# Dispatching tokens to experts by scattering rows into per-expert DRAM regions, block by block

## The chip, the cores and the metric

One core of a Trainium2 chip runs the whole program. The metric is the device time of one execution in microseconds (us); of several runs the median is taken. The engines are named as in the profile: PE (TensorE, matrix multiply), DVE (VectorE), ACT (ScalarE), POOL (GpSimd) and SP (SyncE, which here only issues DMAs). Each engine takes its own instructions in order, so an instruction that waits holds up all that stand behind it on the same engine.

## The reference

Two transformer layers with adaptive layer norm over 2048 tokens of 128 channels, fp32. The part that the change touches is the second half of layer 0, a mixture of experts:

```
x = x + ga * attention0(h)                      # 16 heads of 8, no mask
h = layernorm(x) * (1 + cb) + sb
logits = h @ router_w.T                         # 16 experts
top_vals, top_idx = top_k(logits, 1)            # one expert per token
scores = sigmoid(scattered top_vals)            # 0 for the experts not chosen
routed_in = h * scores                          # per expert
gate, up = split(routed_in @ gate_up_proj)      # 128 -> 2 x 128 per expert
expert_sum = sum over experts of (up * silu(gate)) @ down_proj
shared = silu(h @ shared_gate_w.T) * (h @ shared_up_w.T) @ shared_down_w.T   # 512 wide
x = x + gb * (shared + expert_sum)
```

Layer 1 follows with causal attention (8 heads of 16 that share one key and value head) and a channel mix with a one-token shift.

## The kernel before, in words

The tokens are kept transposed as channels by tokens (`hT`) for matrix products, and as 16 tiles of 128 tokens (`x`) for everything by row. The 2048 tokens are also seen as four blocks of 512 (`b` = 0 to 3).

**Attention 0.** The work is cut into 16 units, one for each block of queries and group of four heads. Each unit has a first pass, 32 steps that compute scores (L377) and take their maximum (L381), and a second pass, 32 steps that compute the scores again with the maximum subtracted (L442), exponentiate (L452) and weigh the values (L468). The order is written by hand: while the second pass of unit u runs, the first pass of unit u+1 is issued between its steps, 8 steps (`LEAD`) ahead. At the end of a first pass the function `turn` transposes the maxima, ACT copies them (`mT`, L411), and two DMAs on the SP queue (L414) write them into rows of the stacked queries `qS`. The scores of the unit's second pass read those rows, so they wait for these two DMAs. The queries of block 1 are put into `qS` by 32 further SP DMAs (`project_q`, lines at L260), issued in the first pass of unit 1. In unit 1's second pass SP also writes zeros (L358) when unit 0's scores are all done.

A list `late` holds small pieces of other work. One is taken off it every other step, and every step in the last unit. It starts with one piece (`fold0`); in the last unit it gets the pieces of `route(b)` for blocks 0 to 2, and those of block 3 run after the unit. `route(b)` normalises block b, transposes it, computes the router's logits (L707), the largest logit `top`, and a one-hot choice `mine` (L714).

**The expert stage.** Rows of `h` are transposed, multiplied with the sigmoid of `top` and written to DRAM (`hs_rows`, L782, SP). A second path works out where each token goes: 17 matmuls of `mine` with triangular and all-one matrices give its position inside its expert (`pos`, L842 to L846), DVE makes from the counts the number of 128-row tiles of each expert and their first slot (`over`, `base`, L851 to L858), and 16 matmuls (L890) invert this to a table `tok` of the token in every slot. There are 31 tiles (`SLOTS`), enough for any split of 2048 tokens over 16 experts. POOL then issues 31 indirect DMAs (L912), each gathering 128 rows of `hs_rows` by `tok`; slots that no token fills read row 0. Eight quads of four tiles follow: transposes of the rows (L921), gate and up products with the expert's weights (L935), the activation (L804 to L806), the down product (L948) and a copy to `y` (L952), stored by SP to `y_rows` (L953). The expert's number of each tile is read into a register of PE, one load per tile (L929). Pieces of the shared expert (L826, L814) are put between the quads. At the end 16 indirect DMAs (L970) gather each token's row of `y_rows` and add it to `x`. The gate `gb` is folded into both down weights by two POOL multiplications (L791).

SP issues its DMAs in order, over eight rotating completion counters: a DMA that reuses a counter first waits until the DMA eight places before it has landed.

Of the kernel before, what the change touches and what calls it, by code (L numbers as in the profile page):

```python
# [18 lines left out]
P = 128  # L19
# [10 lines left out]
SHARED_FIRST = 4  # L30
LEAD = 8
# [11 lines left out]
def two_layers(ctx: ExitStack, tc: tile.TileContext, a: dict, out: bass.AP):  # L43
# [91 lines left out]
    for i, at in enumerate((ident.rearrange("p (r c) -> p r c", c=4)[:, :, 2:4],  # L135
# [4 lines left out]
    nc.gpsimd.memset(zeros, 0.0)  # L140

# [4 lines left out]
    units = const.tile([P, P], F32, name="units")  # L146
    nc.gpsimd.iota(units, pattern=[[1, P]], base=0, channel_multiplier=0,
                   allow_small_or_imprecise_dtypes=True)
    token = const.tile([P, NT], F32, name="token")
    nc.gpsimd.iota(token, pattern=[[P, NT]], base=0, channel_multiplier=1,  # L150
# [135 lines left out]
    def attention(layer, hT, ngrp, dk, scale, causal, kvp, begin, prepare, wq, bq, folded, ended,  # L286
# [22 lines left out]
        with ExitStack() as s:  # L309
# [10 lines left out]
            def other_bank():  # L320
                return banks[(weighing + 1) % 2]
# [209 lines left out]
            if not folded:  # L531
                late.append(lambda: folded.extend(fold0(other_bank())))

# [160 lines left out]
    ranked = const.tile([P, NT, NE], F32, name="ranked")  # L694
    best = const.tile([P, NT], F32, name="best")
    mine = const.tile([P, NT, NE], F32R, name="mine")

    def route(b, bank):
        got = []
        cols = slice(HOFF + b * QB, HOFF + (b + 1) * QB)  # L700
        ts = slice(b * TB, (b + 1) * TB)

        def choose():
            ps = bank()[:, :TB * NE].rearrange("p (t e) -> p t e", e=NE)
            for i in range(TB):
                lo = HOFF + b * QB + i * P
                nc.tensor.matmul(ps[:, i, :], h1[:, lo:lo + P], wr0, start=True, stop=True)  # L707
            nc.vector.tensor_reduce(top[:, ts], ps, AX.X, ALU.max)
            r = ranked[:, ts, :]
            nc.vector.tensor_tensor(r, ps, top[:, ts].unsqueeze(2).to_broadcast([P, TB, NE]),  # L710
                                    ALU.is_equal)
            nc.vector.tensor_tensor(r, r, rank.unsqueeze(1).to_broadcast([P, TB, NE]), ALU.mult)
            nc.vector.tensor_reduce(best[:, ts], r, AX.X, ALU.max)
            nc.vector.tensor_tensor(mine[:, ts, :], r,  # L714
                                    best[:, ts].unsqueeze(2).to_broadcast([P, TB, NE]),
                                    ALU.is_equal)

        return [lambda: got.extend(moments(b, f"ln1{b}")),
                lambda: got.append(normal(b, f"ln1{b}", *got)),
                lambda: turn_normal(bank(), got[2], h1[:, cols], m[:, 4:5], m[:, 3:4]),  # L720
                choose]
# [10 lines left out]

    def ended0(bank):
        return ([lambda: folded1.extend(fold_gate(const, bank(), wo1, vcol(V_BP),
                                                  mods[1][:, 2:3], "a1"))]
                + [p for b in range(NB - 1) for p in route(b, bank)])
# [3 lines left out]
    a0.close()  # L740

# [14 lines left out]
    with ExitStack() as s:  # L756
# [10 lines left out]
        topsig = rp.tile([P, NT], F32, name="topsig")  # L767
        nc.scalar.activation(topsig, top, AF.Sigmoid)


        hs = rp.tile([P, NT, P], F32, name="hs")
        hs_v = a["hs_rows"].rearrange("(t p) c -> p t c", p=P)
        for b in range(NB):
            ps = pt.tile([P, QB], F32, name=f"hs_ps{b}", tag="t")
            for i in range(TB):
                t = b * TB + i
                nc.tensor.transpose(ps[:, i * P:(i + 1) * P], hT[:, t * P:(t + 1) * P], ident)
            for i in range(TB):
                t = b * TB + i
                nc.scalar.activation(hs[:, t, :], ps[:, i * P:(i + 1) * P], AF.Copy,  # L780
                                     scale=topsig[:, t:t + 1])
            nc.sync.dma_start(out=hs_v[:, b * TB:(b + 1) * TB, :],  # L782
                              in_=hs[:, b * TB:(b + 1) * TB, :])

# [4 lines left out]
        nc.scalar.copy(gb, ps[:, :P])  # L789
        for w, n in ((wsd, NS), (wdn, NE)):  # L790
            nc.gpsimd.tensor_tensor(w, w, gb.unsqueeze(1).to_broadcast([P, n, P]), ALU.mult)  # L791
# [5 lines left out]
        def silu_up(ps, n, name):  # L797
# [6 lines left out]
            nc.scalar.activation(v[0], g, AF.Sigmoid)  # L804
            nc.vector.tensor_tensor(v[0], v[0], g, ALU.mult)
# [27 lines left out]
        def shared_step():  # L833
            up = shared_up()
            if waiting:
# [3 lines left out]
        first = [shared_up()]  # L839


        pos = pt.tile([P, NT + 1, NE], F32, name="pos_ps", tag="t")  # L842
        nc.tensor.matmul(pos[:, :NT, :], before_r, mine, start=True, stop=False,
                         skip_group_check=True)
        for t in range(NT):
            nc.tensor.matmul(pos[:, t + 1:, :], ones_r,  # L846
                             mine[:, t:t + 1, :].to_broadcast([P, NT - t, NE]),
                             start=False, stop=(t == NT - 1), skip_group_check=True)
        first.append(shared_up())
        over = rp.tile([P, NE, NE], F32, name="over")  # L850
        nc.vector.tensor_tensor(over, pos[:, NT, :].unsqueeze(2).to_broadcast([P, NE, NE]),  # L851
# [7 lines left out]
        place = rp.tile([P, NT, NE], F32, name="place")  # L859
        nc.vector.tensor_tensor(place, pos[:, :NT, :],  # L860
                                base.unsqueeze(1).to_broadcast([P, NT, NE]), ALU.add)
        nc.vector.tensor_tensor(place, place, mine.bitcast(F32), ALU.mult)
        slot = rp.tile([P, NT], F32, name="slot")
        nc.vector.tensor_reduce(slot, place, AX.X, ALU.add)
        slot_i = rp.tile([P, NT], I32, name="slot_i")
        nc.vector.tensor_copy(slot_i, slot)
        hi_i = rp.tile([P, NT], I32, name="hi_i")
        nc.vector.tensor_scalar(hi_i, slot_i, 7, 7, ALU.arith_shift_right, ALU.arith_shift_left)
        hi = rp.tile([P, NT], F32, name="hi")
        nc.vector.tensor_copy(hi, hi_i)  # L870
        lo = rp.tile([P, NT], F32, name="lo")
        nc.vector.tensor_tensor(lo, slot, hi, ALU.subtract)


        NSL = SLOTS + 1
        in_tile = rp.tile([P, NT, NSL], F32, name="in_tile")
        nc.vector.tensor_tensor(in_tile, hi.unsqueeze(2).to_broadcast([P, NT, NSL]),
                                iota[:, :NSL].unsqueeze(1).to_broadcast([P, NT, NSL]),
                                ALU.is_equal)
        in_tile_r = rp.tile([P, NT, NSL], F32R, name="in_tile_r")  # L880
        nc.vector.tensor_tensor(in_tile_r, in_tile,
                                token.unsqueeze(2).to_broadcast([P, NT, NSL]), ALU.mult)
        at = rp.tile([P, NT, P], F32R, name="at")
        ps = pt.tile([P, NSL], F32, name="tok_ps", tag="t")
        for b in range(NB):
            cols = slice(b * TB, (b + 1) * TB)
            nc.vector.tensor_tensor(at[:, cols, :], lo[:, cols].unsqueeze(2).to_broadcast([P, TB, P]),
                                    units.unsqueeze(1).to_broadcast([P, TB, P]), ALU.is_equal)
        for t in range(NT):
            nc.tensor.matmul(ps, at[:, t, :], in_tile_r[:, t, :], start=(t == 0),  # L890
                             stop=(t == NT - 1))
        tok = rp.tile([P, NSL], U32, name="tok")
        nc.vector.tensor_copy(tok, ps)

# [3 lines left out]
        nth = rp.tile([1, SLOTS], F32, name="nth")  # L898
        nc.vector.tensor_reduce(nth, passed[:, :, 1:], AX.X, ALU.add)
        expert = rp.tile([1, SLOTS], I32, name="expert")  # L900
        nc.vector.tensor_copy(expert, nth)

        for up in first:
            shared_act(*up)
# [4 lines left out]
        quads = [list(range(j, min(j + TB, SLOTS))) for j in range(0, SLOTS, TB)]  # L909
        xs = rp.tile([P, SLOTS, P], F32, name="xs")  # L910
        for j in range(SLOTS):
            nc.gpsimd.indirect_dma_start(  # L912
                out=xs[:, j, :], out_offset=None, in_=a["hs_rows"],
                in_offset=bass.IndirectOffsetOnAxis(ap=tok[:, j:j + 1], axis=0))
        y_v = a["y_rows"].rearrange("(j p) c -> p j c", p=P)
        xsT, gup, acts, actT, regs = {}, {}, {}, {}, {}
# [9 lines left out]
        def gathered(q):  # L926
            xsT[q] = turned([xs[:, j, :] for j in quads[q]], len(quads[q]), f"xsT{q}")
            for j in quads[q]:
                regs[j] = nc.tensor.value_load(expert[0:1, j:j + 1], min_val=0, max_val=NE - 1)  # L929
# [14 lines left out]
        def down(q):  # L944
# [7 lines left out]
            nc.vector.tensor_copy(y[:, :n, :].rearrange("p j f -> p (j f)"), ps[:, :n * P])  # L952
# [53 lines left out]
        def bank():  # L1006
            return pt.tile([P, QB], F32, name="a1bank", tag="t")
# [122 lines left out]
```

## Time and profile before

| what | value |
| --- | --- |
| median of 3 runs | 1295.77 us (1295.49 to 1297.65) |
| the profiled execution's own time | 1296.39 us |
| span of the profiled execution, first to last instruction | 1294.7 us |
| mean granted PE clock | 0.933 |
| PE busy | 1166.7 us (90%) |
| DVE busy | 958.2 us (74%) |
| ACT busy | 776.4 us (60%) |
| POOL busy | 112.3 us (9%) |
| bytes moved by DMA | 27.38 MB |

The span starts with loads and the first norm, attention 0 fills about 92 to 812 us, the router of the last block and the expert stage about 812 to 978 us, then attention 1 and the channel mix follow. All times in the text count from the start of the span. Busy shares are averages over these stages, so what a part of the change is worth has to be read in its own stage. A name like `a0qS<-a0mT` in a line gives what is written and what is read, and `<-` behind an idle time gives what ended it. In the rows by stretch of time, each engine's busy us stand with their number of instructions, then the granted clock, the mean busy share of the 16 DMA engines, and GB/s.

### The profile page before, as it was taken

The numbers are of one execution on the slowest core, as the hardware profiler recorded it, in microseconds if no ns is written. First come the engines' busy times: TensorE is split into PE (matmuls) and PEld (weight loads), VectorE is DVE, ScalarE is ACT, GpSimd is POOL, SyncE is SP. The second block draws the span as 40 slices with busy tenths as digits, with TensorE's granted clock in tenths as the row PEclk, the third lists the DMA queues.
The fourth block names the chain that finished last, engine by engine and source line by source line (L and its number), as shares of the span: only waits on it lengthen the run. The fifth ranks groups of instructions, "written<-read, shape, count | busy, mean of one in ns | idle before, by whom it ended". The sixth has DMA issues, their size and how long they took to land.

```text
span 1294.7 us, 22355 instructions
## 1 busy us (share of the span) xinstructions
PE 1166.7 (90%) x9243; PEld 528.8 (41%) x9243; DVE 958.2 (74%) x1494; ACT 776.4 (60%) x857; POOL 112.3 (9%) x173
## 2 busy tenths in 40 slices
PE   5579999999999999999999999854977999999986
PEld 3233443444334344334434434533643444444432
DVE  4788888989888898898898841531468779897225
ACT  6117777777777777777777787401312355656763
POOL 2010000000000000000000000253041111100113
PEclk9659999999999999999999999876976799999998
DMA  4831000000000010000000000413211001000001
GB/s 127 112 37 34 3 2 2 2 19 18 1 2 2 3 34 2 2 2 2 2 2 1 2 2 1 131 38 34 57 31 33 19 15 29 7 1 1 2 1 32
DMA packets 25317, 27.38 MB, mean 21 GB/s; under 512 B 5328, under 2 KB 18896, under 8 KB 24704
## 3 DMA queue, kind: packets, MB, share of 16 engines
q1 hardware_dynamic: 21440, 20.50, 7.4%
q0 software_dynamic: 1504, 3.08, 1.6%
q10 hardware_dynamic: 2272, 2.36, 0.8%
q8 instruction: 73, 1.20, 0.4%
q14 instruction: 28, 0.23, 0.1%
HBM read 9.88 MB, written 4.13 MB: 11 GB/s over the span
## 4 chain that ended last, share of the span: by engine, by line
PE 77%; DVE 11%; ACT 4%; issue 3%; another core or an unknown queue 2%; DMA 1%; POOL 1%; POOLq 0%; ACTq 0%; DVEq 0%; SPq 0%
PE a0bank L468 23%; PE a0p L442 17%; PE a0p L377 12%; PE a1bank L468 5%; PE a1p L442 4%; DVE a0mx L381 3%; PE a1p L377 2%; DVE a1mx L381 2%; PE a1p L448 2%; DVE a1masked L386 2%; PE sg L826 2%; ACT a0e L452 1%; PE gu L935 1%; PE a0bank L499 1%
## 5 line engine op out<-in xcount | busy, mean ns | idle before, releaser
L381 DVE TENSOR_REDUCE a0mx<-a0p 128x2 f32<-128x1024 f32 x512 | 623.6, 1224 | 78.0 <-PE a0p L377 68.4
L452 ACT ACTIVATE a0e<-a0p 128x1024 f32<-128x1024 f32 x512 | 521.7, 1024 | 172.5 <-PE a0p L442 147.2
L468 PE MATMUL a0bank<-a0e,vA 128*32 128x256 f32 x4096 | 333.6, 392 | 0.6 <-ACT a0e L452 0.6
L377 PE MATMUL a0p<-kS,a0qS 64*128 64x512 f32 x1024 | 248.2, 481 | 26.4 <-DVE a0mx L381 13.4
L442 PE MATMUL a0p<-a0qS,kS 64*128 64x512 f32 x1024 | 259.8, 497 | 0.0
L452 ACT ACTIVATE a1e<-a1p 128x1024 f32<-128x1024 f32 (+3 forms) x160 | 143.1, 896 | 97.4 <-PE a1p L448 94.4
L442 PEld LDWEIGHTS a0p<-a0qS,kS 64*128 64x128 f32 x1024 | 97.1, 184 | 204.3 <-issue 128.8
L377 PEld LDWEIGHTS a0p<-kS,a0qS 64*128 64x128 f32 x1024 | 100.3, 192 | 111.3 <-ACT a0e L452 58.1
L468 PEld LDWEIGHTS a0bank<-a0e,vA 128*32 128x32 f32 x4096 | 86.4, 108 | 139.2 <-issue 124.9
L381 DVE TENSOR_REDUCE a1mx<-a1p 128x2 f32<-128x1024 f32 x96 | 115.6, 1222 | 20.8 <-PE a1p L377 19.9
L468 PE MATMUL a1bank<-a1e,vA 128*32 128x256 f32 (+1 forms) x1152 | 97.5, 385 | 0.5 <-POOL a1e L455 0.4
L442 PE MATMUL a1p<-a1qS,kS 64*128 64x512 f32 (+3 forms) x320 | 76.4, 472 | 3.1 <-DVE a1mx L381 1.9
L377 PE MATMUL a1p<-kS,a1qS 64*128 64x512 f32 (+3 forms) x320 | 68.3, 429 | 7.1 <-DVE a1mx L386 4.1
L386 DVE CUSTOM_DVE_ANT_0 a1masked<-a1p,later 128x128 f32<-128x128 f32 (+3 forms) x128 | 62.5, 489 | 13.3 <-PE a1p L377 8.5
L977 POOL MEMSET vA<- 128x16 f32 x1 | 0.1, 128 | 718.4 <-PE a0bank L520 718.4
L448 PE MATMUL a1p<-a1mT,a1ones 64*128 64x512 f32 (+3 forms) x320 | 61.8, 378 | 0.0
L442 PEld LDWEIGHTS a1p<-a1qS,kS 64*128 64x128 f32 x320 | 31.1, 190 | 60.9 <-issue 33.4
L377 PEld LDWEIGHTS a1p<-kS,a1qS 64*128 64x128 f32 x320 | 32.7, 199 | 36.1 <-DVE a1mx L386 10.3
L455 POOL TENSOR_SCALAR_AFFINE_SELECT a1e<-a1e 128x256 f32<-128x256 f32 x64 | 26.0, 406 | 233.7 <-ACT a1e L452 233.7
L468 PEld LDWEIGHTS a1bank<-a1e,vA 128*32 128x32 f32 x1152 | 25.4, 108 | 43.0 <-issue 32.8
L935 PE MATMUL gu<-wgu_sb,xsT 128*128 x62 | 18.5, 451 | 20.0 <-issue 19.5
L411 ACT CAST a0mT<-a0bank 8x512 fp32r<-8x512 f32 x16 | 9.2, 574 | 45.4 <-PE a0bank L410 45.3
(330 smaller groups left out, 795.7 us busy)
## 6 DMA issues: line engine op xcount, KB each, us to landing
kS<-a0qS SPq DMA_DIRECT2D x28, 128.0 KB
wgu_sb<-in_gate_up SPq DMA_DIRECT2D x1, 2048.0 KB
a0qS<-a0qh SPq DMA_DIRECT2D x62, 32.0 KB
a0qS<-a0ql SPq DMA_DIRECT2D x62, 32.0 KB
y_rows<-y SPq DMA_DIRECT2D x7, 256.0 KB
a1qS<-a1qh SPq DMA_DIRECT2D x24, 64.0 KB
a1qS<-a1ql SPq DMA_DIRECT2D x24, 64.0 KB
hs_rows<-hs SPq DMA_DIRECT2D x4, 256.0 KB
```

What stands on the lines that cost most here:

```text
L377: nc.tensor.matmul(ps[:, j, :n], qS[b][r:r + RT, st, i * P:(i + 1) * P], kS(st)[r:r + RT, kb * QB:kb * QB + n], start=True, stop=True)
L381: nc.vector.tensor_reduce(pm[:, i, 2 * pair:2 * pair + 2, kb], ps, AX.X, ALU.max)
L386: nc.vector.tensor_tensor_reduce(masked[:, :n], ps[:, j, :n], later[:, QB - n:], 1.0, LOWEST, ALU.add, ALU.max, pm[:, i, g, kb:kb + 1])
L411: nc.scalar.copy(mT, ps[:nm_rows])
L442: nc.tensor.matmul(ps[:, j, q0:], kS(st)[r:r + RT, kt * P:(kt + 1) * P], qS[b][r:r + RT, st, q0:], start=True, stop=fused)
L448: nc.tensor.matmul(ps[:, j, q0:], ones[r:r + RT, g // S, :], shift[u][r:r + RT, q0:], start=False, stop=True)
L452: nc.scalar.activation(e[:, :, q0:], ps[:, :, q0:], AF.Exp, scale=scale)
L455: nc.gpsimd.affine_select(out=e[:, :, q0:q0 + P], in_=e[:, :, q0:q0 + P], compare_op=ALU.is_ge, fill=0.0, base=0, pattern=[[0, 2], [1, P]] ...
L468: nc.tensor.matmul(av[g * W:(g + 1) * W, c0:c1], vA(kt, grp * HG + g), held[kt, g // 2][:, g % 2, c0:c1], start=(kt == 0 and c0 == 0), sto ...
L499: nc.tensor.transpose(ps[:, i * P:(i + 1) * P], o[:, i * P:(i + 1) * P], ident)
L826: nc.tensor.matmul(ps[:, j, :], w[:, k * P:(k + 1) * P], hT[:, b * QB:(b + 1) * QB], start=True, stop=True)
L935: nc.tensor.matmul(ps[:, i, :], xsT[q][:, i * P:(i + 1) * P], wgu[:, bass.ds(regs[j], 1), :].rearrange("p a f -> p (a f)"), start=True, st ...
```

## The change

The tables that say which token is in which slot are gone. Instead DRAM holds `sent`, 17 regions of 2048 rows, the first 16 for the experts and the last one spare. As soon as a block's experts are chosen, its rows are transposed, scaled, and scattered by four indirect POOL DMAs to expert times 2048 plus position (`place` and `send`, two more pieces per block). `sent` must hold zeros where nothing is scattered, so 68 SP DMAs of 256 KB (`clear`) write zeros over it, as 17 pieces of four on the `late` list of attention 0, in program order on SP. In SP's order the first four stand before the 32 DMAs of `project_q(1)`, the next 40 between these and the two DMAs of unit 1's maxima (L414 of before), and the other 24 before those of unit 2's.

After the last scatter, SP reads 31 start addresses into registers and loads 31 tiles of 128 consecutive rows from `sent`; POOL's 31 gathers are gone. PE reads all experts' numbers in one load. Of each expert's region only as many 128-row tiles are read as its tokens fill; the tiles that are left over read on behind those of the last expert, for which the spare region leaves room. The sigmoids are written with tanh: sigmoid(z) = 0.5 tanh(z/2) + 0.5, and the missing factor 0.5 of silu is put into `gb`. The routed down weights are no longer multiplied with `gb`; the copy to `y` becomes a multiplication with it.

```diff
+    blank = const.tile([P, P], F32, name="blank")
+    nc.gpsimd.memset(blank, 0.0)
...
             if not folded:
                 late.append(lambda: folded.extend(fold0(other_bank())))
+                late.extend(pieces0())
...
+            nc.scalar.activation(topsig[:, ts], top[:, ts], AF.Tanh, scale=0.5)
+            nc.vector.tensor_scalar(topsig[:, ts], topsig[:, ts], 0.5, 0.5, ALU.mult, ALU.add)
+
+        def place():
+
+            ps = bank()[:, :(TB + 1) * NE].rearrange("p (t e) -> p t e", e=NE)
+            nc.tensor.matmul(ps[:, :TB, :], before_r, mine[:, ts, :], start=True, stop=False,
+                             skip_group_check=True)
+            for i in range(TB):
+                t = b * TB + i
+                nc.tensor.matmul(ps[:, i + 1:, :], ones_r,
+                                 mine[:, t:t + 1, :].to_broadcast([P, TB - i, NE]),
+                                 start=False, stop=(i == TB - 1), skip_group_check=True)
+            r = lnp.tile([P, TB, NE], F32, name=f"place{b}", tag="ranked")
+            nc.vector.tensor_tensor(r, ps[:, :TB, :],
+                                    at[b].unsqueeze(1).to_broadcast([P, TB, NE]), ALU.add)
+            nc.vector.tensor_tensor(r, r, mine[:, ts, :].bitcast(F32), ALU.mult)
+            nc.vector.tensor_reduce(row[:, ts], r, AX.X, ALU.add)
+            nc.vector.tensor_copy(row_i[:, ts], row[:, ts])
+            nc.vector.tensor_tensor(at[b + 1], at[b], ps[:, TB, :], ALU.add)
+
+        def send():
+
+            ps = bank()
+            for i in range(TB):
+                lo = HOFF + b * QB + i * P
+                nc.tensor.transpose(ps[:, i * P:(i + 1) * P], h1[:, lo:lo + P], ident)
+            hs = lnp.tile([P, TB, P], F32, name=f"hs{b}", tag="xn")
+            nc.vector.tensor_tensor(hs, ps.rearrange("p (t c) -> p t c", c=P),
+                                    topsig[:, ts].unsqueeze(2).to_broadcast([P, TB, P]), ALU.mult)
+            for i in range(TB):
+                t = b * TB + i
+                nc.gpsimd.indirect_dma_start(
+                    out=sent[t], in_=hs[:, i, :], in_offset=None,
+                    out_offset=bass.IndirectOffsetOnAxis(ap=row_i.bitcast(U32)[:, t:t + 1],
+                                                         axis=0))
...
-                choose]
+                choose, place, send]
...
+    def clear(n):
+
+        rows = a["sent"].rearrange("(n p r) c -> n p r c", p=P, r=CLEAR)
+        tc.keep_in_program_order(nc.sync.dma_start(
+            out=rows[n], in_=blank.unsqueeze(1).to_broadcast([P, CLEAR, P])))
+
+    def pieces0():
+        return [lambda n=n: [clear(CLEARS * n + i) for i in range(CLEARS)]
+                for n in range((NE + 1) * T // (P * CLEAR * CLEARS))]
...
-        nc.scalar.activation(topsig, top, AF.Sigmoid)
...
-        for w, n in ((wsd, NS), (wdn, NE)):
-            nc.gpsimd.tensor_tensor(w, w, gb.unsqueeze(1).to_broadcast([P, n, P]), ALU.mult)
+        nc.scalar.activation(gb, ps[:, :P], AF.Copy, scale=0.5)
+        nc.gpsimd.tensor_tensor(wsd, wsd, gb.unsqueeze(1).to_broadcast([P, NS, P]), ALU.mult)
...
-            nc.scalar.activation(v[0], g, AF.Sigmoid)
-            nc.vector.tensor_tensor(v[0], v[0], g, ALU.mult)
+            nc.scalar.activation(v[0], g, AF.Tanh, scale=0.5)
+            nc.vector.scalar_tensor_tensor(v[0], v[0], 1.0, g, ALU.add, ALU.mult)
...
+        starts = registers(0, mybir.EngineType.SP, (NE + 1) * T - P)
...
+        for j in range(SLOTS):
+            nc.sync.dma_start(out=xs[:, j, :], in_=a["sent"][bass.ds(starts[j], P), :])
...
-        for j in range(SLOTS):
-            nc.gpsimd.indirect_dma_start(
-                out=xs[:, j, :], out_offset=None, in_=a["hs_rows"],
-                in_offset=bass.IndirectOffsetOnAxis(ap=tok[:, j:j + 1], axis=0))
+        regs = registers(1, mybir.EngineType.PE, NE - 1)
...
-            nc.vector.tensor_copy(y[:, :n, :].rearrange("p j f -> p (j f)"), ps[:, :n * P])
+            nc.vector.tensor_tensor(y[:, :n, :],
+                                    ps[:, :n * P].rearrange("p (j f) -> p j f", f=P),
+                                    gb.unsqueeze(1).to_broadcast([P, n, P]), ALU.mult)
```

Gone with the tables are the 16 transposes and four stores of `hs_rows`, the 17 matmuls of `pos` and the 16 of `tok_ps`; the count of rows of each expert now comes from the running starts `at`. The first two pieces of the shared expert move behind these tables.

## Prediction

> **What bounds the kernel now.** I read the page first: PE is busy 90% of the span and carries 77% of the chain that ended last. So a stage in which PE idles is where time can be won, and a wait put into a full stage costs its whole length.
>
> ```profile
> PE 1166.7 (90%) x9243; PEld 528.8 (41%) x9243; DVE 958.2 (74%) x1494; ACT 776.4 (60%) x857; POOL 112.3 (9%) x173
> PE 77%; DVE 11%; ACT 4%; issue 3%; another core or an unknown queue 2%; DMA 1%; POOL 1%; POOLq 0%; ACTq 0%; DVEq 0%; SPq 0%
> ```
>
> Second, the busy time by stretch, for the places where the change acts: attention 0 where the zeros are written, its last unit, and the expert stage.
>
> ```profile
> 100.00:110.00 10.00, 10.00 (x94) 3.79 (x92) 8.84 (x8) 7.04 (x8) 0.00 (x0) 0.97 0.21 49
> 120.00:130.00 10.00, 10.00 (x89) 4.18 (x88) 9.48 (x11) 7.34 (x9) 0.00 (x0) 1.00 0.05 11
> 770.00:800.00 30.00, 30.00 (x264) 13.67 (x261) 5.31 (x22) 23.84 (x28) 0.00 (x0) 1.00 0.01 2
> 866.00:886.00 20.00, 0.98 (x9) 0.74 (x7) 0.79 (x2) 1.18 (x2) 15.13 (x17) 0.65 0.37 49
> 900.00:933.00 33.00, 28.73 (x174) 23.00 (x173) 15.46 (x25) 11.16 (x20) 0.00 (x0) 1.00 0.17 46
> ```
>
> Attention 0 is full on PE (10.00 of 10, 30.00 of 30) with the DMA engines nearly idle. The expert stage has a hole: from 866 to 886 PE works 0.98 of 20 us, and only POOL, issuing gathers, is busy. From 900 on PE is full again.
>
> Third, the chain of waits through that stage:
>
> ```profile
> 835.53 3.19 DVE over L855
> 849.44 1.17 POOL xs L912
> 858.22 3.75 PE gu L935 x8
> 864.09 13.50 another core or an unknown queue
> 878.20 4.28 another core or an unknown queue
> 885.89 7.10 another core or an unknown queue
> 893.79 2.05 PE y_ps L948 x8
> 901.83 1.99 PE gu L935 x8
> 914.15 1.99 PE gu L935 x8
> ```
>
> Routing of the last block ends with `mine` at 828.5 us; the first gather is issued at 849.44, the first expert product starts at 858.22, the third quad's only at 885.9. Two quads then take 914.15 − 901.83 = 12.3 us, 6.2 each.
>
> Fourth, SP's own timeline around the place where the zeros go:
>
> ```profile
> 84.04 1.23 SPq L414 DMA_DIRECT2D a0qS<-a0mT  x2
> 119.76 1.22 SPq L260 DMA_DIRECT2D a0qS<-a0ql  x2
> 130.57 1.14 SPq L414 DMA_DIRECT2D a0qS<-a0mT  x2
> 136.20 1.85 SPq L358 DMA_DIRECT2D a0qS<-zeros  x2
> ```
>
> `project_q(1)` leaves SP at 121.0. The maxima of unit 1 go out at 130.6; unit 0's scores end at 136.2 (what L358 waits for), and unit 1's scores follow. So these maxima have some 3 to 5 us to spare.
>
> **The change, part by part.** *Zeros, first 40.* They stand on SP between `project_q(1)` and unit 1's maxima. SP is not gated by the steps that the pieces were hung on, only by landings: it issues them from 121.0 as fast as eight in flight land. 40 × 262,144 B = 10.49 MB. The rate, by stores of the same form (512 B rows from 128 partitions) and by the saturated loads:
>
> ```profile
> 932.00:934.00 2.00, 2.00 (x16) 1.76 (x16) 1.38 (x3) 0.59 (x1) 0.00 (x0) 1.00 0.49 131
> 3.00:6.00 3.00, 0.00 (x0) 0.00 (x0) 1.23 (x8) 1.49 (x2) 3.00 (x22) 1.00 1.12 347
> ```
>
> The `y_rows` store moves 131 GB/s at a share of 0.49: 267 at a full share, 39.3 us for the 40. The loads reach 347: 30.2 us. The Trainium skill ("DMA: Bandwidth & Descriptors", Specifications) gives about 358 GB/s to HBM per core, an estimate of 29.3 us. The stores are the nearest row, but packets overlap when saturated (share 1.12), so I take 290, 36 us. The maxima then land at 121 + 36 + 1.5 = 158.5, needed at 136.5: PE stands 22 us, ACT and DVE with it. It restarts at half clock: a step took 2.16 us at 0.5 against 1.35 warm (96.8 to 98.9 us), and the clock rose after about 4 us of it, so +2. Sum **+24**; by the skill's rate +17, by 267 GB/s +28. The first four zeros (85 to 89 us) lie in SP's gap before 99.67: nothing. The last 24 take 22 us of the 44.8 until the next maxima: nothing, unless a clear takes over 1.8 us. The skill speaks against the change here: "Issuing engines are not separate DMA queues" of the same page says that all issuers share the 16 engines, so another issuer would not make the zeros cheaper; it is their order before the maxima that costs.
>
> *`place` and `send` of blocks 0 to 2*, in the last unit, where PE is full and a step takes 1.12 us: per block four transposes (0.66, as L229 x4 there) and five small matmuls (about 0.5, from 0.12 each in `pos`), 3.5 us for three, with bank waits **+4.5** (3 to 8). DVE (5.31 of 30) and POOL are free there.
>
> *The way to the first tile.* From `mine` at 828.5: five matmuls, four DVE operations of 0.22 and waits, row numbers at about 832.8; hs needs 0.7 us on DVE beside it; POOL scatters at 835 to 839.6 (1.17 + 3 × 1.25, as the gathers), landed at 842 (2.5 as "DMA xs" at 854.66). Beside it the counts reach registers: DVE operations without the 3.2 us of `over` (0.42 as its equals, when POOL doesn't multiply beside it), about 842. SP's load of 31 registers: the row for one on PE is 0.30 us, so 0.3 to 9.3; the skill ("Runtime: NRT & Kernel Launch") says about 200 ns per register "even for bulk", 6.2. I take 6. The tiles go out at 848, land from 850, and gu(q0) starts at 852.5: **−6** (−8 to +2). 31 loads at 0.65 us are not the bound (four in 2.6 us against 6.2 per quad); at SP's 1.2 us they'd still pass.
>
> *The hole.* Data were there: gu(q1) ended at 866.2 and its four gathers had landed, yet ACT's activation began at 877.6. The wait is put down to no queue. It ends with POOL's run of gathers (888.1), whose last stretch shows engines busy at few bytes:
>
> ```profile
> 882.00:890.00 8.00, 3.57 (x8) 2.52 (x8) 0.00 (x0) 0.58 (x1) 4.71 (x5) 0.55 0.89 42
> ```
>
> A share of 0.89 at 42 GB/s is packets that wait; unused slots all read row 0. Without gathers I expect it gone. Then eight quads at 6.2 from 852.5 end at 902.1, plus 1.5 for a cold first quad (3.75 against 1.99 us for eight gu) 903.6, against 932.65 for the last y_ps of before: **the stage gives −29**, the first tile's −6 and one cold restart less within it; −22 to −34, the further end if DVE without the old tables runs the quads closer to PE's own work. Nothing behind it is nearer to its limit: the sixteen yx gathers (936.8 to 956.5) stay as they are and move along.
>
> *Small ones.* `y` times `gb` costs a copy's 0.69; scalar_tensor_tensor likewise; POOL's 4.55 us multiplication was seen only through `over`: counted. Tanh for sigmoid saves a table load (1.28 us at 819, where ACT is idle anyway) and one more at attention 1: **−1**.
>
> Sum: 24 + 4.5 − 29 − 1 = −1.5 on the 1296.4 of the profiled execution, which stands 0.6 above the median: 1294.3. With all terms at their good ends (17 + 3 − 34 − 1) −15, at their bad ends (28 + 8 − 22 − 1) +13. Two large terms cancel, so the sign hangs on the size of each.
>
> **The rivals.** *A, the zeros hide.* If stores saturate well above 347 GB/s, or SP gets to the zeros earlier than I read, the exposed part falls to 8 or less: 8 + 4.5 − 29 − 1 = −17.5, 1278; with nothing exposed 1270. For it: a store's share of 0.49 is no saturated queue, so its rate there isn't known. Against: 347 is the most that any stretch shows, and at that rate the zeros end 15 us too late.
>
> *B, the hole stays.* If it comes not from the gathers but from something that PE's and ACT's streams keep (PE's register loads, or what "unknown queue" covers), the stage gives only the first tile's −6: 24 + 4.5 − 6 − 1 = +21.5, 1317, slower. It decides as soon as more than a few us of the hole are left. For it: PE was idle with its data there, which a slow gather doesn't explain. Against: the hole ends when POOL's run ends.
>
> *C, the zeros cost more.* My 36 us are 0.90 us a clear. From 0.94 the sum is above zero, from 1.0 above what can be measured; at 1.25 (210 GB/s) PE stands 36 + 2 us: 38 + 4.5 − 29 − 1 = +12.5, 1308, slower. For it: the same 64 KB of zeros are read from the partitions again and again, a pattern that no row shows. Against: the stores' 267.
>
> **How the numbers follow.** Main case (hole gone, zeros exposed for 17 to 28) 0.60, its own range 1281 to 1309; of it 0.29 is faster, 0.09 the same, 0.22 slower, as its centre lies 1.5 below and its good end is as far off as its bad. A 0.18, faster; B 0.15 and C 0.07, slower. 0.2% is 2.6 us, about what a measurement of this kernel can tell from no change. Faster 0.47, same 0.09, slower 0.44. The number is the main case's 1294. The range, 1268 to 1319, leaves out the far end of A, and what B and C would give together.
>
> **What would show it.** Right: SP's rows of the zeros end at about 157, and unit 1's maxima right behind them; PE idle about 20 us from 136 on, put down to a DMA of `a0mT`; clock 0.5 after it; attention 0 ends at about 840. From the last `mine` to the first gu 24 us instead of 29.7, no empty stretch between quads, 75 us from `mine` to the last y_ps instead of 104. Wrong: no idle PE at 136 (A), an empty stretch behind the second quad again (B), or a clear above 1.05 us (C).

## The result and the profile after

The changed kernel takes 1291.62 us (median of 8 runs, 1288.68 to 1295.98) against 1297.18 us before in the same comparison: a ratio of 0.996, with a 95% interval of 0.9943 to 0.9978. The forecast was 1294. The small gain is what is left of two large amounts of opposite sign, and the profiles show both. The profiled execution of the changed kernel took 1295.98 us, the slowest of its eight runs, so its own end understates the gain; the stages are compared inside the traces.

**The cost: attention 0.** SP's timeline of the changed kernel, where a line gives start, duration, queue, line and what is written from what:

```profile
85.01 1.24 SPq L416 DMA_DIRECT2D a0qS<-a0mT  x2
...
121.71 35.61 SPq L779 DMA_DIRECT2D sent<-blank  x40
157.42 1.57 SPq L416 DMA_DIRECT2D a0qS<-a0mT  x2
159.04 20.91 SPq L779 DMA_DIRECT2D sent<-blank  x24
180.05 1.52 SPq L360 DMA_DIRECT2D a0qS<-zeros  x2
198.66 1.09 SPq L416 DMA_DIRECT2D a0qS<-a0mT  x2
```

The 40 zero stores hold SP from 121.7 to 157.3, 0.89 us each, and the two DMAs with the maxima of unit 1 stand behind them until 157.4 (130.6 before). The next maxima go out at 198.7 instead of 175.3, 23.3 us later; 1.0 of these was there at the first maxima already (85.01 against 84.04), so the stall costs 22.3. In the busy times by stretch PE is empty and the clock goes to half, with the DMA engines full:

```profile
130.00:140.00 10.00, 9.65 (x97) 3.99 (x98) 8.24 (x7) 7.03 (x8) 0.00 (x0) 1.00 1.02 288
140.00:150.00 10.00, 1.03 (x12) 0.42 (x4) 0.55 (x2) 0.59 (x1) 0.00 (x0) 0.76 1.02 287
150.00:160.00 10.00, 0.00 (x0) 0.00 (x0) 0.00 (x0) 0.00 (x0) 0.00 (x0) 0.50 0.96 276
160.00:170.00 10.00, 9.21 (x48) 3.64 (x48) 6.03 (x5) 5.07 (x6) 0.00 (x0) 0.55 0.99 278
```

PE's waits from 130 to 165 us name it (what waited, for what; us in total, times, longest):

```profile
PE a0p L444 <- DMA a0qS<-a0mT: 18.8, 1, 18.8
```

**The gain: the expert stage.** The chain of waits of the changed kernel, from the last block's scatters to the third quad:

```profile
865.60 0.99 POOL sent L756
...
869.42 1.56 POOL sent L756
871.00 1.29 POOL wsd_sb L826
872.34 3.62 PE sum L849 x16
875.98 0.69 DVE acts L841
...
876.96 2.08 SPq L906
...
885.24 1.78 DMA xs<-sent
...
887.17 3.75 PE gu L956 x8
...
894.02 1.74 PE gu L956 x8
...
896.91 1.99 PE gu L956 x8
```

The third quad's gate and up products (gu) follow those of the second by 3 us (894.0, 896.9), where before they came 22 us later (864.2, 885.9): the hole is gone. Times between events, each from its own trace:

| stretch | before | after | difference | forecast |
| --- | --- | --- | --- | --- |
| first maxima to unit 2's maxima on SP | 91.3 | 113.7 | +22.3 | +24 |
| last unit's maxima (763.3, 786.5) to the last block's normalised rows (822.5, 852.0) | 59.2 | 65.5 | +6.3 | +4.5 |
| last `mine` (828.4, 858.6) to first gu (858.2, 887.2) | 29.9 | 28.6 | −1.2 | −6 |
| first gu to the end of the last y_ps (932.7, 929.8) | 74.4 | 42.7 | −31.8 | −23 |

At the end of the last y_ps the traced execution of the change is 2.8 us ahead of that of before, while the medians are 5.6 us apart; the traces don't show where the other 2.8 us lie.

### The profile page after: what moved, and what is told of

It reads as the page before. It is cut to its first block, busy times and chain, and to the rows that moved or that the text cites. A ratio compares the mean times of both kernels' runs of the same rounds, so it can differ in the third digit from the quotient of the medians.

```text
span 1294.3 us, 22407 instructions
## 1 busy us (share of the span) xinstructions
PE 1169.2 (90%) x9230; PEld 529.1 (41%) x9230; DVE 960.4 (74%) x1519; ACT 771.4 (60%) x842; POOL 95.0 (7%) x157
## 4 chain that ended last, share of the span: by engine, by line
PE 76%; DVE 10%; SPq 5%; ACT 4%; issue 2%; POOL 2%; DMA 2%; POOLq 0%; ACTq 0%; DVEq 0%; another core or an unknown queue 0%
PE a0bank L470 22%; PE a0p L444 16%; PE a0p L379 12%; PE a1bank L470 6%; PE a1p L444 4%; DVE a0mx L383 3%; SPq L779 3%; PE a1p L379 2%; PE a1p L450 2%; DVE a1mx L383 2%; PE sg L861 2%; DVE a1masked L388 1%; SPq L262 1%; ACT a0e L454 1%; PE gu L956 1%
## 5 line engine op out<-in xcount | busy, mean ns | idle before, releaser
L444 PE MATMUL a0p<-a0qS,kS 64*128 64x512 f32 x1024 | 261.8, 500 | 18.8 <-DMA a0qS<-a0mT 18.8
L756 POOL DMA_INDIRECT sent<-hs,row_i x16 | 16.4, 1022 | 743.6 <-DVE ln11xn L224 712.8
L839 ACT ACTIVATE sigs<-sg 128x512 f32<-128x512 f32 x16 | 9.5, 597 | 43.8 <-PE sg L861 32.9
```

Of the source, the lines that this page charges most:

```text
L444: nc.tensor.matmul(ps[:, j, q0:], kS(st)[r:r + RT, kt * P:(kt + 1) * P], qS[b][r:r + RT, st, q0:], start=True, stop=fused)
L756: nc.gpsimd.indirect_dma_start(out=sent[t], in_=hs[:, i, :], in_offset=None, out_offset=bass.IndirectOffsetOnAxis(ap=row_i.bitcast(U32)[:, ...
```

## The experiments

The numbers are medians, and the ratio of each to the kernel before with its 95% interval. The kernel before ran beside each of them, with medians from 1294.9 to 1297.2 us, so small differences between rows are read from the ratios.

| kernel | us | ratio, interval |
| --- | --- | --- |
| the change | 1291.6 | 0.996 (0.9943 to 0.9978) |
| e1, zeros later | 1270.7 | 0.978 (0.9757 to 0.9805) |
| e2, before with the zeros alone | 1314.1 | 1.014 (1.0114 to 1.0162) |
| e3, before, empty slots read their own rows | 1296.8 | 1.000 (0.9984 to 1.0024) |
| e4, before, one load of the experts | 1296.3 | 1.000 (0.9984 to 1.0006) |
| e5, the change with loads by tile | 1297.7 | 1.001 (0.9998 to 1.0023) |
| e6, zeros later and gate folded early | 1263.4 | 0.976 (0.9709 to 0.9808) |
| e7, before, 12 gathers | 1268.9 | 0.978 (0.9725 to 0.9835) |
| e8, before, 12 gathers and 19 unread ones | 1296.0 | 1.000 (0.9987 to 1.0020) |
| e9, before, gathers paced | 1283.9 | 0.990 (0.9871 to 0.9922) |
| e10, the change with sigmoid | 1289.8 | 0.994 (0.9907 to 0.9973) |
| e11, e9 with one load of the experts | 1280.2 | 0.988 (0.9851 to 0.9910) |
| e12, e6 with PE's load moved ahead | 1266.2 | 0.979 (0.9767 to 0.9814) |

**What the zeros cost.** e1 leaves all 68 of them but hangs them behind unit 1's maxima:

```diff
-CLEAR, CLEARS = 4, 4
+CLEAR, CLEARS = 4, 2
...
+                late.extend([lambda: None] * 11)
                 late.extend(pieces0())
```

> The changed kernel with the zeros hung two by two behind the maxima of units 1, 2 and 3 instead of four by four from the start (32, 32 and 4 of them). Theory 1, that the order of the 40 zeros before unit 1's maxima on SP costs the 23 us by which attention 0 ends later: the maxima of unit 1 go out at about 131 us again, the 32 zeros behind them take 28 us (0.89 each) and are done before the next maxima at 175, no PE idle time is put down to a0mT, and the time falls from 1291.6 to 1268 to 1272. Rival, that it is the zeros' traffic itself that slows attention 0: the idle time moves to another unit and the time stays above 1283.

Measured 1270.7, 21 us under the change. SP's timeline of e1:

```profile
132.69 1.14 SPq L416 DMA_DIRECT2D a0qS<-a0mT  x2
133.88 28.93 SPq L780 DMA_DIRECT2D sent<-blank  x32
...
176.49 1.09 SPq L416 DMA_DIRECT2D a0qS<-a0mT  x2
177.63 29.25 SPq L780 DMA_DIRECT2D sent<-blank  x32
```

The same stores at 0.90 to 0.91 us each now end 13.7 us before the next maxima, and no PE wait for `a0mT` is left. While they are written, PE stays full at full clock with the DMA engines full:

```profile
140.00:150.00 10.00, 10.00 (x94) 3.86 (x86) 9.13 (x8) 8.22 (x9) 0.00 (x0) 1.00 1.01 286
```

So their traffic costs nothing to attention 0; their place in SP's order costs the stall.

e2 adds only the zeros to the kernel before, with `clear` and `pieces0` copied from the change.

> The kernel before with only the zeros added, at the place where the change puts them, and nothing that reads them. Theory 1: PE idles 19 to 20 us at 139 and restarts at half clock, the next maxima go out at 198.7 instead of 175.3, and the time is 1297 + 23 = 1320. Rival, that part of the stall is made up later (a slack behind attention 0): below 1312.

Measured 1314.1, 1.4% or 17 us more, not 23, and so between the two expectations. In its trace the stall is there in full (maxima at 156.6, then 197.3; PE waits 17.8 us for `a0mT`), and it is still 21 us at the yx gathers (958.2 against 936.8). The profiled run then took 299.3 us from attention 1's first scores to the output stores, where before and the change took 305.5 and 306.8. Nothing in this stage was changed. Runs of one kernel differ by several us (last section), but with one trace for each kernel it isn't shown that this stage is where they differ; what made up for 6 us here stays open.

**What the hole was.** In the kernel before, three results of PE that its records end by 867 (first group of lines) are taken up by ACT at 877.6, 885.3 and 893.1 (second group), 11, 19 and 26 us later. `remote` is a release that the profile puts down to no engine.

```profile
864.19 1.97 PE L935 MATMUL gu<-wgu_sb,xsT 128*128 x8
865.99 0.49 PE L921 MATMUL xsT_ps<-ident,xs 128*128 128x128 f32 x3
866.32 0.60 PE L921 MATMUL actT_ps<-ident,acte 128*128 128x128 f32 x4
```

```profile
877.61 0.60 ACT L804 ACTIVATE sige<-gu 128x512 f32<-128x512 f32 x1 [12.94 <-remote]
885.30 0.58 ACT L923 COPY xsT<-xsT_ps 128x512 f32<-128x512 f32 x1 [7.10 <-issue]
893.07 0.58 ACT L923 COPY actT<-actT_ps 128x512 f32<-128x512 f32 x1 [7.18 <-remote]
```

PE waits for ACT's two copies: for the first with the third quad's gu (885.9), for the second with the first down product (893.8). No instruction fetch lies behind the hole. Instructions come by DMA too (queues of kind `instruction` in the trace), but from 866 to 893 only the gathers' queue moved anything (packets, MB, share of the 16 engines), and the next fetch follows at about 904.

```profile
q0 software_dynamic: 601, 1.25, 48.9%
```

The forecast put the hole to the gathers. Three readings were possible: the slow packets of row 0, PE's loads in the same stretch, or the run of gathers itself. e3 takes away the first:

```diff
+        beyond = rp.tile([P, NT], F32, name="beyond")
+        nc.vector.tensor_tensor(beyond, token, lo, ALU.subtract)
...
-                                token.unsqueeze(2).to_broadcast([P, NT, NSL]), ALU.mult)
+                                beyond.unsqueeze(2).to_broadcast([P, NT, NSL]), ALU.mult)
...
-        nc.vector.tensor_copy(tok, ps)
+        nc.vector.tensor_scalar_add(tok, ps, token[:, 0:1])
```

> The kernel before, but a slot that no token fills reads row p of hs_rows in partition p instead of row 0 (one more DVE operation of 0.2 us, nothing else). Theory 2, that the hole of 866 to 886 us comes from all these slots reading one row: the third quad's gu starts at 868 to 872 instead of 885.9, the slow packets at the end of the gathers go, and the time falls by 10 to 18 us to 1279 to 1287. Rival, that the hole has another cause (PE's register loads, POOL's run of gathers as such): the same hole, 1296 to 1299.

Measured 1296.8: the same. The slow packets did go; the stretch 886 to 890 has a DMA share of 0.94 at 41 GB/s in before (first line) and 0.19 at 49 in e3 (second). But e3's third quad starts at 884.5 after 16.9 us of idle PE. Reading one row kept the DMA engines busy, and it was not what made the hole.

```profile
886.00:890.00 4.00, 3.51 (x8) 2.46 (x8) 0.00 (x0) 0.00 (x0) 1.75 (x2) 0.60 0.94 41
886.00:890.00 4.00, 2.29 (x6) 1.30 (x4) 0.00 (x0) 0.00 (x0) 2.20 (x3) 0.50 0.19 49
```

e4 takes away the second:

```diff
-            for j in quads[q]:
-                regs[j] = nc.tensor.value_load(expert[0:1, j:j + 1], min_val=0, max_val=NE - 1)
...
+        regs = nc.values_load_multi_w_load_instructions(
+            expert[0:1, :], engines=[mybir.EngineType.PE], min_val=0, max_val=NE - 1,
+            skip_runtime_bounds_check_because="a sum of at most 15 comparisons")[1]
```

> The kernel before, but PE reads all experts' numbers by one load in front of the first quad instead of one load per tile. Theory 3, that the loads by tile hold PE: they are 31 times 0.30 us with a register operation and a check each, so if each holds PE's queue the quads after 900 go from 12.3 us a pair to about 10.2, as in the changed kernel, and the time falls by 6 to 10 us; if the hole too comes from these loads, by 20 or more. Rival, that the loads are hidden: 1296 to 1299, 12.3 us a pair.

Measured 1296.3, the same, but not for the rival's reason. The pairs of quads did shrink, to 9.9 us (907.31 to 917.24). The hole stayed, here in the first four quads:

```profile
865.89 3.75 PE L937 MATMUL gu<-wgu_sb,xsT 128*128 x8 [2.79 <-issue]
873.41 1.89 PE L937 MATMUL gu<-wgu_sb,xsT 128*128 x8
897.45 3.78 PE L937 MATMUL gu<-wgu_sb,xsT 128*128 x8 [21.05 <-ACT xsT L927]
907.31 1.89 PE L937 MATMUL gu<-wgu_sb,xsT 128*128 x8
```

Counted from the last `mine`, its first gu came 5.1 us later than before's (35.0 us against 29.9), right behind the load of 2.3 us (863.2 to 865.5), and its third quad 9.0 us later (66.5 against 57.6). So the 7 us won in three pairs filled a longer wait.

e7 and e8 take the run itself. In e7 POOL gathers only the first 12 tiles, and SP fills the other 19 with other rows; e8 adds the 19 gathers again, into a tile that nothing reads. Cuts from e7's edit, then from e8's addition:

```diff
-        for j in range(SLOTS):
+        for j in range(12):
             nc.gpsimd.indirect_dma_start(
...
+        for j in range(12, SLOTS):
+            nc.sync.dma_start(out=xs[:, j, :],
+                              in_=a["hs_rows"][(j % NT) * P:(j % NT + 1) * P, :])
```

```diff
+        spare = rp.tile([P, SLOTS - 12, P], F32, name="spare")
+        for j in range(12, SLOTS):
+            nc.gpsimd.indirect_dma_start(
+                out=spare[:, j - 12, :], out_offset=None, in_=a["hs_rows"],
...
```

> The kernel before with only the first 12 gathers on POOL; the other 19 tiles are loaded by SP from 128 consecutive rows of hs_rows, so their contents and the output differ from the reference. Theory 5, that the hole comes with POOL's long run of gathers: the run ends near 864.5, before the hole began, the hole is gone, the third quad's gu starts by 870, and the time is 15 to 20 us under before (1277 to 1282). Rival 5b, that the hole lies in what PE, ACT and DVE do at the second quad: gu of the third quad at 884 to 887 all the same, 1295 to 1299.

> As the kernel with twelve gathers, so with another output, but POOL still issues the other 19 gathers, into a tile that nothing reads. If the run of gathers as such makes the hole (theory 5): the hole is back, the third quad's gu at 884 to 887 and 1295 to 1299. If the hole needs quads that wait for late gathers (5c): as with twelve gathers, 1277 to 1282.

Measured 1268.9 and 1296.0. The first gu lines of e7, then of e8:

```profile
858.67 3.57 PE L938 MATMUL gu<-wgu_sb,xsT 128*128 x8 [0.57 <-issue]
864.46 1.97 PE L938 MATMUL gu<-wgu_sb,xsT 128*128 x8
867.92 1.99 PE L938 MATMUL gu<-wgu_sb,xsT 128*128 x8 [0.66 <-ACT xsT L926]
874.97 1.99 PE L938 MATMUL gu<-wgu_sb,xsT 128*128 x8 [0.24 <-DVE acte L806]
```

```profile
859.57 3.75 PE L943 MATMUL gu<-wgu_sb,xsT 128*128 x8 [0.57 <-issue]
865.75 1.89 PE L943 MATMUL gu<-wgu_sb,xsT 128*128 x8
883.72 3.78 PE L943 MATMUL gu<-wgu_sb,xsT 128*128 x8 [15.31 <-issue]
...
901.18 1.99 PE L943 MATMUL gu<-wgu_sb,xsT 128*128 x8 [0.24 <-DVE acte L806]
```

This settles it: 19 gathers whose data nobody reads bring the hole back, and with it 27 us. POOL's long run of indirect gathers as such stops the quads. It costs more than the 15 to 20 us forecast, since the hole doesn't end with the third quad. That one comes 15.8 us later in e8 than in e7, and the fourth follows it after 17.5 us instead of 7.1: there too the last of the late results, taken up at 892.9, holds the first down product until 893.7, and PE runs at half clock meanwhile (eight gu in 3.78 us against 1.99).

e9 keeps the whole computation of before and only lets three tiles rotate, so POOL must pause for PE:

```diff
-        xs = rp.tile([P, SLOTS, P], F32, name="xs")
...
+            xs[q] = wp.tile([P, TB, P], F32, name=f"xs{q}", tag="xs")
...
+        for q in range(3):
+            gather(q)
...
+            if q + 3 < len(quads):
+                gather(q + 3)
```

> The kernel before with its gathers and its full computation, but the rows of the quads go into three rotating tiles instead of one, so POOL runs 12 gathers and can issue the next four only when PE has transposed the quad of three before. Theory 5 (a long unbroken run of gathers holds PE's signals): the breaks end it, the third quad's gu starts by 872, and the time is 1268 to 1280. Rival, that what counts is how many gathers were issued in all, or that each further group waits for a quad and is on the path: a hole or late quads from the fourth on, 1285 to 1297.

Measured 1283.9, a gain of 1%, less than expected. POOL's timeline of e9 at its first pause:

```profile
874.33 0.94 POOL L915 DMA_INDIRECT xs<-hs_rows,tok  x1 [0.30 <-issue]
878.81 0.95 POOL L915 DMA_INDIRECT xs<-hs_rows,tok  x1 [3.54 <-remote]
```

and PE's, for what this gather waited for, the third quad's transposes, and for what followed:

```profile
867.05 0.49 PE L927 MATMUL xsT_ps<-ident,xs 128*128 128x128 f32 x3
867.38 0.60 PE L927 MATMUL actT_ps<-ident,acte 128*128 128x128 f32 x4
879.21 3.78 PE L943 MATMUL gu<-wgu_sb,xsT 128*128 x8 [11.23 <-ACT xsT L929]
```

The transposes are recorded by 867.6, and POOL learns of it at 878.8, 3.5 us after the end of its 20th gather in a row. So even POOL sees PE's signal 11 us late. Breaking the run shortened the hole to 11 us. The break also fits a pattern: in before, e2, e3, e4, e8, e9 and e11 ACT's wait for the late results ends 2.5 to 5.0 us after POOL's run of gathers pauses or ends. The ends of matmuls are modelled in the trace, so it can't say whether the matmuls were late or only their signals. By what way the gathers do it, and whether POOL's issuing or the packets are to blame, was not shown.

**What PE's loads cost.** e5 puts the loads by tile of before back into the change:

```diff
-        regs = registers(1, mybir.EngineType.PE, NE - 1)
...
+            for j in quads[q]:
+                regs[j] = nc.tensor.value_load(nth_i[0:1, 1, j:j + 1], min_val=0, max_val=NE - 1)
```

> The changed kernel with PE's register loads of before, one per tile, in place of its single load. Theory 3, that the single load is what shortens the quads from 12.3 us a pair to 10.3: pairs of 12.3 us again, 8 us more over four pairs, less about 2 us for the single load itself that the first quad no longer waits for: 1295 to 1300 against 1291.6. Rival, that the shorter pairs come from the work around them (no pending gathers, the multiplication by gb): pairs stay near 10.3 and the time within 3 us of 1291.6.

Measured 1297.7, 6 us over the change, and the two intervals of the ratio don't overlap. Its pairs of quads, from 903.00 to 915.82 and from 907.64 to 919.95, take 12.8 and 12.3 us, against 10.5 and 10.2 in the change (903.18, 913.66; 906.34, 916.49). So the single load, which the diff shows as a detail, is worth as much as the whole net gain. The trace shows 3.5 of the 6 us by the end of the last y_ps (74.7 us after the last `mine` against 71.3). The 2 us expected back ahead of the first quad didn't come: its gu starts 29.8 us after the last `mine`, 28.6 in the change.

e11 adds the single load to e9.

> The kernel with paced gathers and, in addition, PE's single load of all experts' numbers. If the loads by tile are on the path of full quads (12.3 against 10 us a pair, theory 3): 5 to 8 us below the kernel with paced gathers, 1262 to 1272. Rival, that gathers at 5 us a quad (4 times 1.25) plus their landing now set the pace: no faster than with paced gathers alone.

Measured 1280.2 against 1283.9; their intervals overlap, so a gain of the size expected isn't shown. Its first gu came 35.0 us after the last `mine` instead of 29.5 in e9, as in e4. Of its pairs of quads one takes 14.3 us (889.90 to 904.22; 14.9 in e9) and the next 9.8 (12.2 in e9). The long pair isn't the pace of the gathers that the rival names: the transposes of the activation, recorded by 892.7, are taken up by ACT at 896.2, late again beside POOL's last gathers.

```profile
896.15 0.59 ACT L933 COPY actT<-actT_ps 128x512 f32<-128x512 f32 x1 [0.94 <-remote]
```

**The way to the first tile.** e6 is e1 with the gate folded in the last unit of attention 0, ahead of the scatters:

```diff
+    gb = const.tile([P, P], F32, name="gb")
+
+    def fold_gb(bank):
...
+        nc.gpsimd.tensor_tensor(wsd, wsd, gb.unsqueeze(1).to_broadcast([P, NS, P]), ALU.mult)
...
-        return ([lambda: folded1.extend(fold_gate(const, bank(), wo1, vcol(V_BP),
+        return ([lambda: fold_gb(bank())] + [lambda: folded1.extend(fold_gate(const, bank(), wo1, vcol(V_BP),
...
```

> The kernel with the later zeros, and in addition gb and the multiplication of wsd (1.3 us on POOL) moved into the last unit of attention 0, ahead of the scatters. Theory 4, that in the changed kernel this multiplication, queued behind the last block's four scatters, holds the shared sums (5.4 us of PE), and through an activation ahead of it on DVE the start addresses: nth_i 3 to 4 us earlier after the last mine, first gu 3 to 5 us earlier, 1270.7 falls to 1265 to 1268. Rival, that the way through the scatters and SP's loads is as long: the idle 5.4 us go, the first gu stays 28 us behind the last mine, 1269 to 1272.

Measured 1263.4, the lowest median of all, 2.4% under before; its interval overlaps that of e1, so the times alone don't prove a gain over e1. From the last `mine` to the first gu it takes 24.1 us, 28.4 in e1, and PE's wait for `wsd_sb` (4.3 us in e1, 5.3 in the change) is gone. That is theory 4's 3 to 5 us; the other 3 us between the two medians are not explained by it.

e12 moves PE's load of the experts' numbers ahead of the first quad's transposes.

```diff
+        expert = rp.tile([1, 32], I32, name="expert")
+        nc.vector.tensor_copy(expert, nth[:, 1, :])
...
+                if name == "xsT0" and i == 0:
+                    tc.keep_in_program_order(turn)
```

> The kernel with the later zeros and the early multiplication, and in addition PE's load of the experts' numbers placed ahead of the first quad's transposes (from a tile of its own, which is ready before the start addresses) instead of behind them. Theory 7, that the 2.9 us of idle PE ahead of the first gu, which the waits put down to a DMA of xs, are this load (2.3 us, issued when the transposes were done): the idle time goes, the load lies in the wait for the first tiles, first gu about 2 us earlier after the last mine (24.1 to about 22), 1261 to 1262. Rival, that the DMA is what is waited for: first gu unchanged, 1262.5 to 1265.

PE's waits of e6 in this stage, and the lines of the load in e6 and e12 (duration in ns, then first and last start):

```profile
PE gu L960 <- DMA xs<-sent: 2.9, 1, 2.9
```

```profile
L910 PEldq TENSOR_LOAD <-nth_i x1: 2317/2317/2317, 856.7 to 856.7; - x1
```

```profile
L912 PEldq TENSOR_LOAD <-expert x1: 2321/2321/2321, 853.4 to 853.4; - x1
```

In e6 the load runs from 856.7 to 859.0 and gu starts at 859.28; the wait that is put down to a DMA is the load. In e12 it lies under the wait for the first tiles, the 2.9 us are gone, and from the end of SP's own load to the first gu it takes 5.1 us instead of 7.9. (From the last `mine` it takes 19.2 us against 24.1, but in e12's trace `mine` itself came 2.4 us later after the last maxima.) Its time is no proof of a gain: 1259.3 to 1271.1 over four runs, with an interval that overlaps e6's.

**Tanh.** e10 is the change with sigmoids:

```diff
-            nc.scalar.activation(topsig[:, ts], top[:, ts], AF.Tanh, scale=0.5)
-            nc.vector.tensor_scalar(topsig[:, ts], topsig[:, ts], 0.5, 0.5, ALU.mult, ALU.add)
+            nc.scalar.activation(topsig[:, ts], top[:, ts], AF.Sigmoid)
...
-            nc.scalar.activation(v[0], g, AF.Tanh, scale=0.5)
-            nc.vector.scalar_tensor_tensor(v[0], v[0], 1.0, g, ALU.add, ALU.mult)
+            nc.scalar.activation(v[0], g, AF.Sigmoid)
+            nc.vector.tensor_tensor(v[0], v[0], g, ALU.mult)
...
```

> The changed kernel with the sigmoids of before (for the router's value and for silu) instead of tanh; gb is not halved. Theory 6, that tanh only saves table loads where ACT has time: the three blocks routed in the last unit switch tables between exponentials, up to six loads of 1.28 us with ACT busy 24 of 30 us there, of which 2 to 5 us reach PE, one more load at attention 1 and none in the quads: 1293 to 1298 against 1291.6. Rival, that the loads stand on the path of full steps: six times 1.3 and their drains, over 1300.

Measured 1289.8 against 1291.6, and the intervals overlap: no cost, against both expectations. The trace shows the table loads coming back, 13 of 1.28 us instead of 5, six of them between 808 and 834. From the last unit's maxima to the last block's normalised rows it takes 66.3 us against 65.5, so ACT's slack there takes nearly all of them.

## Why the prediction was right, and where it was only lucky

- *Zeros, +24.* 22.3 measured: 18.8 us are PE's wait (22 forecast), the other 3.5 fall into the restart (2 forecast), with a granted clock of 0.55 from 160 to 170. The rate was chosen between 267 and 347 GB/s at 290; SP's 40 stores moved 10.49 MB in 35.61 us, 294 GB/s, and the maxima went out at 157.4 where 157 was forecast. The estimate of 29.3 us from the Trainium skill's figure ("DMA: Bandwidth & Descriptors", Specifications) was too short; the trace's stores were the better guide. Rivals A and C fall with it, and e1 shows the mechanism. No run gave the zeros another issuer. That the engines are shared, as the prediction argues, does not speak against it: e1 shows that the order on SP and not the traffic cost the time.
- *`place` and `send`, +4.5.* 6.3 measured, inside the stated 3 to 8.
- *The first tile, −6.* Only −1.2. The step that failed: POOL's remaining multiplication, counted only through `over`, was queued behind the scatters, held PE's sums by 5.3 us and through an activation ahead of it on DVE the start addresses (the chain above, 871.0 to 876.7); they were there 18.2 us after the last `mine` instead of 13.5. From the first tile's load on SP to the first gu it took 7.7 us instead of 4.5, with PE's own load of 2.3 us in it. In the other direction, SP's load of the registers was put at 6 us and took 2.08. The skill's price of about 200 ns per register ("Runtime: NRT & Kernel Launch", Instruction fetch mechanics), which that page gives for loads from HBM, doesn't fit this load of 32 from an SBUF tile, 65 ns each.
- *The hole.* That the gathers made it was right (e7, e8); the reason given beside it, slots that all read row 0, was wrong (e3), and the hole lasted until 893.1, 5 us longer than POOL's run. Rival B falls.
- *The quads, 6.2 each.* They took 42.7 us from first gu to the end of the last y_ps instead of the 51.1 that the forecast's steps add up to. The sum left out that the change turns PE's 31 loads by tile into one; e5's time puts 6 us on them, its trace 3.5, and what made the rest isn't shown. This term was better than forecast by 8.5 us and the first tile's worse by 4.8, and their sum hid it: −33 for the stage against −29.
- *Small ones, −1.* Nothing is to be seen of it (e10).

So the mechanisms of the two large terms, the stall behind the zeros and the hole that goes with the gathers, were right, and the size of the stall with them. That the sum came so near was luck: the errors of the four terms, −1.7, +1.8, +4.8 and −8.5 us, cancelled in part.

## What to carry to other kernels

A DMA that no one waits for still costs time when a DMA that the critical engine needs stands behind it on the same issuing engine: here 35.6 us of stores cost 22.3. Order the issues by what is needed next, and work out what one period of the schedule can hold. A stretch in which engines idle with their data there is to be tested by taking away its neighbour's activity, not only its own inputs: 19 unread gathers told more here than any view of the trace. And a single register load ahead of a loop is worth counting as carefully as a matmul: PE's took 2.3 us.

## What the runs showed of the hardware that was not expected

- With 20 (e9) or 31 (before, e8) indirect gathers of 128 rows in a row on POOL, one each 1.25 us, other engines took up PE's results 11 to 26 us after their recorded ends, with little traffic (49 GB/s from 866 to 886 in before). Twelve in a row (e7) did not do it; numbers between were not run.
- A load of 32 registers took 2.08 us on SP and 2.32 us on PE; a load of one took 0.30.
- Gathers whose unused slots all read one row kept the DMA engines busy at a share of 0.94 with 41 GB/s; with a row for each partition it was 0.19 with 49.
- Runs of one kernel differ by several us: before from 1286.3 to 1299.5 over 39 runs, and its two fastest, 1286.3 and 1286.4, had the highest mean granted clocks, 0.940 and 0.942. At the start of attention 1 the traces of two kernels with the same code there differ in the clock (the changed kernel has 0.52, 0.50 and 0.61 from 981 to 1011; e2 in the same stage 0.63, 0.50 and 0.85); what sets it isn't shown.
